# First layer of a four-layer network: transforms beside attention, mixing products beside attention, a late broadcast and weights laid out by the host

## Chip, cores and metric

The kernel runs on one core of one Trainium2 chip. The metric is the device time of one execution in microseconds. The profile shows five engines: PE (TensorE, with its weight loads as PEld), DVE (VectorE), ACT (ScalarE), POOL (GpSimd) and SP (SyncE, which here only issues DMAs). Each engine takes its instructions in the order of its own list; DMAs go through queues that SP, ACT and POOL fill.

## What is computed

The reference is a network of four layers on an input of 4 x 64 images of 128 x 128, each layer a mixing part ("conv") and a second part ("ffn"). The change concerns the mixing part of the first layer, and one constant of the second layer. Cut to what matters:

```python
tokens = x.reshape(B * C, 1, H, W)                # 256 images of 128 x 128
tn = inorm(tokens, n1_g, n1_b)
k, q = fno1(tn, k_spec, k_sw, k_sb, (64, 64)), fno1(tn, q_spec, ...)   # 8 heads, low modes at half size
v = fno1(tn, v_spec, v_sw, v_sb, (128, 128))
attn = softmax(einsum('batm,basm->bats', q, k) / sqrt(m))              # over the 64 images of a batch
out = einsum('bats,basm->batm', attn, v)
a = inorm(fno1(out, p_spec, p_sw, p_sb) + tokens, an_g, an_b)
an = inorm(a, n2_g, n2_b)
h = gelu(inorm(spectral_conv(an, m1_spec)) + conv1x1(an, m1_sw, m1_sb))
h = inorm(spectral_conv(h, m2_spec)) + conv1x1(h, m2_sw, m2_sb)
o = inorm(h, mo_g, mo_b) + a
```

`fno1` is a product of the low Fourier modes with complex weights, plus a pointwise weight; `inorm` normalises an image by its own mean and variance.

## The kernel before

The 256 images are two groups of 128 (two batches each). `l0_conv` (L286) does for each group g first `forward(g)` (L322) and then `attention(g, ...)` (L480), in the order forward(0), attention(0), forward(1), attention(1); the tile scheduler orders the instructions of each engine from this program, and it may start blocks of forward(1) early, where their buffers are free. Then `l0_mixer` (L633) does everything that follows the attention.

`forward(g)` goes over 16 blocks of 8 images. For a block SP loads the images into `xt` (L332, 512 KB); DVE takes their statistics (L179 ff.) and with ACT normalises them into `tt` (L344, L348); POOL's queue writes `tt` to the DRAM tensor `tokens` (L351); PE multiplies each image with the matrix `fx` (L356); ACT copies the low modes to `ylow` (L357) and more modes to `yb` (L358); PE multiplies `yb` with `fg` (L362) and DVE copies the result to `rr` (L366). After the 16 blocks PE makes the low modes in both directions, `c32`, from `ylow` (64 accumulated products), and a Gram matrix from `rr` (32 products, `ghigh`). These two need the whole group.

Once, beside forward(0), small weights of q, k, v and p are loaded on SP's queue, combined by DVE on 8 partitions, written to DRAM (`dq`, `dk`, `dem`) and read back as broadcasts (`wq`, `wk`, later `em`). The constants of the mixer are loaded on SP's queue too, among them four weight tiles `m1_w0` to `m2_w1` (113 x 32): each is set to zero and filled by four DMAs that gather 17 x 32 single elements (L602).

`attention(g)`: 14 DVE products `qt`, `kt` (L491–498); for each of nine heads six transposes on PE, two ACT copies (L509) and three accumulated products (L513), then a DVE operation (L517); softmax (L537–544); sum over heads `ah` (L549); for each of eight value heads one transpose, an ACT copy, six DVE operations (L532–534) and three products (L562); then 16 groups of four transposes of `om` (L579), each copied to `lc` (L581) and written to the DRAM tensor `modes` by POOL's queue; at the end the matrix `mix[g]` (`at2`, L586).

`l0_mixer` works through a list of steps with costs and due times written by hand (class `Plan`), which decides the order on each engine before the kernel is built. `tokens(0)` loads group 0's normalised images from DRAM into `tk0` (4 DMAs of 2 MB), multiplies each of the 128 columns with `mix[0]` (128 products of 128 x 128 x 128 in 32 groups of four, L847) and copies each group of four back into `tk0` (L851, DVE and ACT in turn). `tokens(1)` does the same for group 1 beside the first blocks. Then 16 blocks of 16 images follow: the low modes `lo` are loaded (L870, on SP's queue), inverse transforms (L791, L804) are added (L875), and two spectral convolutions, GELU, normalisations and the residual (`xt`, loaded on SP's queue, L960) make the output `zz`, which POOL's queue writes to `state` (L987).

Ahead of everything else in POOL's order two DMAs on its queue broadcast a constant of 64 KB to 8 MB each in DRAM (`pk`, L3344); the second layer reads `pk`.

Of the kernel before, what the change touches and what calls it, by code (L numbers as in the profile page):

```python
# [22 lines left out]
P = 128  # L23
# [261 lines left out]

def l0_conv(env, x, out, tscr, prm, cst):  # L286

    nc, tc = env.nc, env.tc
    KCH = ((0, 11), (11, 22), (22, 32))
    with ExitStack() as ctx:  # L290
# [11 lines left out]
        def columns(names, n=None):  # L302
            for k in names:
                a = prm[k]
                a = a.rearrange("a b -> (a b)") if len(a.shape) == 2 else a
                sc[k] = cp.tile([P, n or 1], F32, name=k)
                nc.sync.dma_start(sc[k], a.partition_broadcast(P))

        columns(("n1_g", "n1_b"))
        mix = [cp.tile([P, P], F32, name="at2_%d" % g) for g in range(2)]  # L310
        modes = [dram.tile([KR, 64, P], F32, name="modes%d" % g) for g in range(2)]
        with ExitStack() as mctx:
# [8 lines left out]

            def forward(g):  # L322


                i0 = g * P
                NB = 8
                ylow = ap.tile([P, P, 64], F32, name="ylow")
                rr = ap.tile([P, 32, P], F32, name="rr")
                rv = gp.tile([P, P], F32, name="rv")
                for s0 in range(0, P, NB):  # L330
                    xt = bp.tile([P, NB, C], F32, name="xt")
                    nc.sync.dma_start(xt, x[i0 + s0 : i0 + s0 + NB].rearrange("t w c -> w t c"))  # L332
# [18 lines left out]
                    nc.gpsimd.dma_start(tscr[i0 + s0 : i0 + s0 + NB].rearrange("t w c -> w t c"), tt)  # L351
                    yb = bp.tile([P, NB, P], F32, name="yb")
                    for j in range(0, NB, 2):
# [6 lines left out]
                    for k in range(2):  # L360
                        for r in range(2):
# [3 lines left out]
                            )  # L365
                    nc.vector.tensor_copy(rr[:, :, s0 : s0 + NB], p2.rearrange("k t h -> k h t"))  # L366
                alpha = gp.tile([P, P], F32, name="alpha")
                pa = pst.tile([P, P], F32, name="pg")
# [8 lines left out]
                for k0, k1 in KCH:  # L377
                    p3 = psum.tile([P, 11, 34], F32, name="p3", bufs=1)
                    for k in range(k0, k1):
                        nc.tensor.matmul(p3[:, k - k0, :], ylow[:, :, k], fy[:, 0, :], start=True, stop=False)  # L380
                        nc.tensor.matmul(p3[:, k - k0, :], ylow[:, :, 32 + k], fy[:, 1, :], start=False, stop=True)
                    nc.scalar.activation(c32[:, k0:k1, :], p3[:, 0 : k1 - k0, :], AF.Copy, scale=acol)

                nc.vector.tensor_add(c32[:, 0, 0:1], c32[:, 0, 0:1], sc["n1_b"])
# [7 lines left out]
                nc.vector.tensor_scalar(ghigh, ghigh, b64, None, ALU.add)  # L392
                return c32, ghigh, acol

            first = forward(0)


            columns(("p_sb",))
            columns(("q_sw", "k_sw", "v_sw", "p_sw", "q_sb", "k_sb"), 8)
            mask = const(mp, "mask", [P, P])  # L400
# [78 lines left out]

            def attention(g, c32, ghigh, acol):  # L480
                c16 = ap.tile([P, 2, 16, 9], F32, name="c16")
# [8 lines left out]
                for dst, wgt, sb, k in ((qt, wq, "q_sb", 64.0), (kt, wk, "k_sb", 1.0)):  # L490
                    nc.vector.tensor_mul(dst[:, :, 0, :], wgt[:, :, 0, :], cr)  # L491
                    nc.vector.tensor_mul(tmp, wgt[:, :, 1, :], ci)
                    nc.vector.tensor_sub(dst[:, :, 0, :], dst[:, :, 0, :], tmp)
                    nc.vector.tensor_mul(dst[:, :, 1, :], wgt[:, :, 0, :], ci)
                    nc.vector.tensor_mul(tmp, wgt[:, :, 1, :], cr)
                    nc.vector.tensor_add(dst[:, :, 1, :], dst[:, :, 1, :], tmp)
                    d0 = dst[:, 0:8, 0, 0]
                    nc.vector.scalar_tensor_tensor(d0, sc[sb], k, d0, ALU.mult, ALU.add)

                att = ap.tile([P, 8, P], F32, name="att")  # L500
                for h in (8, 0, 1, 2, 3, 4, 5, 6, 7):
                    qk = []
                    for src in (qt, kt):
                        flat = src[:, h].rearrange("p r m -> p (r m)")
                        pt = psum.tile([96, 3, P], F32, name="p1")
                        for j in range(3):
                            nc.tensor.transpose(pt[:, j, :], flat[:, 96 * j : 96 * j + 96], env.ident)
                        t = bp.tile([96, 3, P], F32, name="qkT" + str(len(qk)))
                        nc.scalar.copy(t, pt)  # L509
                        qk.append(t)  # L510
                    psc = psum.tile([P, P], F32, name="p2")
                    for j in range(3):
                        nc.tensor.matmul(psc, qk[0][:, j, :], qk[1][:, j, :], start=(j == 0), stop=(j == 2))  # L513
                    if h == 8:
                        nc.vector.tensor_sub(ghigh, ghigh, psc)
                    else:
                        nc.vector.scalar_tensor_tensor(  # L517
                            att[:, h, :], ghigh, sqsk[:, h : h + 1], psc, ALU.mult, ALU.add
                        )

                fs = []
# [17 lines left out]
                nc.vector.tensor_reduce(mx, att, AX.X, ALU.max)  # L539
                nc.vector.tensor_sub(att, att, mx.unsqueeze(2).to_broadcast([P, 8, P]))  # L540
                nc.scalar.activation(att, att, AF.Exp)
                nc.vector.tensor_reduce(mx, att, AX.X, ALU.add)
                nc.vector.reciprocal(mx, mx)
# [4 lines left out]
                for h in range(1, 8):  # L548
                    nc.vector.scalar_tensor_tensor(ah, att[:, h, :], pv[:, h : h + 1], ah, ALU.mult, ALU.add)  # L549
                rowa = ap.tile([P, 1], F32, name="rowa")  # L550
                nc.vector.tensor_reduce(rowa, ah, AX.X, ALU.add)

                po = [pst.tile([P, 11, 34], F32, name="po%d" % i) for i in range(2)] + [
                    pst.tile([P, 11, 34], F32, name="pg")]
                for h in range(8):
# [5 lines left out]
                    for (k0, k1), o in zip(KCH, po):  # L561
                        nc.tensor.matmul(o[:, 0 : k1 - k0, :], aT, f[:, k0:k1, :], start=(h == 0), stop=(h == 7))  # L562
                om = ap.tile([P, 2, 32, KR], F32, name="om")
                nc.gpsimd.memset(om, 0.0)
# [10 lines left out]
                for r in range(2):  # L575
                    for k0 in range(0, 32, 4):
# [4 lines left out]
                        (nc.scalar.copy if (k0 // 4) % 2 else nc.vector.tensor_copy)(lc, pt)  # L581
                        nc.gpsimd.dma_start(modes[g][:, 32 * r + k0 : 32 * r + k0 + 4, :], lc)

                pt = psum.tile([P, P], F32, name="p1")
                nc.tensor.transpose(pt, ah, env.ident)
                nc.vector.scalar_tensor_tensor(mix[g], pt, acol, env.ident, ALU.mult, ALU.add)  # L586

            attention(0, *first)
            attention(1, *forward(1))


# [4 lines left out]
        for n in ("m1", "m2"):  # L596
            for r in range(2):
                w = cp.tile([KH, 32], F32, name="%s_w%d" % (n, r))
                nc.vector.memset(w, 0.0)
                src = prm[n + "_spec"][0, 0, :, :, r].rearrange("a b -> b a")  # L600
                for q in (0, 32, 64, 96):
                    nc.sync.dma_start(w[q : q + 17, :], src)  # L602

# [25 lines left out]

        l0_mixer(env, x, out, tscr, mix, modes, fx, k, sc)  # L630


def l0_mixer(env, x, out, tscr, mix, modes, fx, k, sc):  # L633

# [7 lines left out]
    with tc.tile_pool(name="l0y", bufs=1) as yp, tc.tile_pool(name="l0m", bufs=DEEP) as sb, tc.tile_pool(name="l0s", bufs=DEEP) as sm, tc.tile_pool(  # L642
# [187 lines left out]
        def tokens(g):  # L830
            tk = yp.tile([P, W, C], F32, name="tk%d" % g)
            plan.block()

            def load(q):
                return lambda: nc.sync.dma_start(
                    tk[:, 32 * q : 32 * q + 32, :], tscr[P * g : P * g + P, 32 * q : 32 * q + 32, :])

            for q in range(4):
                step("sp", 0.1, "", "tk%d" % q, load(q), late=15.0 * (q + 1))

# [19 lines left out]
        def block(g, y, made, s0, par):  # L860
# [10 lines left out]

            step("sp", 0.2, "", "lo", load_modes, new="lo gate", late=4.0)

            def add_low(t0, pb):
# [114 lines left out]

        made = [tokens(0)]  # L990
        for g in range(2):
# [2332 lines left out]
def metaformer(tc, a, out, cst):  # L3324

    with ExitStack() as ctx:
# [14 lines left out]
        f0, f2 = part("L0_ffn_"), part("L2_ffn_")  # L3341
        l0_conv(env, x, state[0], tokens, part("L0_conv_"), cst)
        for g in range(2):
            nc.gpsimd.dma_start(  # L3344
                pk[g][0 : P * W * W, :].rearrange("(t f) o -> t (f o)", t=P), cst["l1c_diag"].partition_broadcast(P)
            )
        rnn_ffn(env, state[0], state[1], f0["W"], f0["VT"], f0["gamma"], f0["beta"])
# [35 lines left out]
```

## Time and profile before

| | |
|---|---|
| median of 3 runs | 12344.46 us (12342.34 to 12349.65) |
| profiled execution: time | 12343.01 us |
| profiled execution: span on the core | 12340.9 us |
| mean granted TensorE clock | 0.786 |
| DVE, ACT, PE, POOL busy over the span | 81%, 61%, 61%, 50% |
| first layer's mixing part | 0 to about 1642 us |
| forward(0): last write to `tokens` issued | 235.86 us |
| attention(1): last DVE operation starts | 603.28 us |
| first low modes added in the mixer (L875) | 722.76 us |
| writes to `state` of the 7th, 8th and 16th block | 1151.00, 1231.08, 1636.59 us |

In a timeline row the columns are the start, the busy time, the engine and line, the operation, the tiles out<-in with their sizes, and in brackets the idle time of the engine before it with what ended it. SPq rows are DMA issues; a merged row of several (x16) spans them all. In a window row the columns are the window and its length, then for each engine the busy time with the number of instructions, the granted TensorE clock (1.00 is full speed), the mean busy share of the DMA engines, and GB/s.

### The profile page before, as it was taken

The numbers are of one execution on the slowest core, as the hardware profiler recorded it, in microseconds if no ns is written. First come the engines' busy times: TensorE is split into PE (matmuls) and PEld (weight loads), VectorE is DVE, ScalarE is ACT, GpSimd is POOL, SyncE is SP. The second block draws the span as 40 slices with busy tenths as digits, with TensorE's granted clock in tenths as the row PEclk, the third lists the DMA queues.
The fourth block names the chain that finished last, engine by engine and source line by source line (L and its number), as shares of the span: only waits on it lengthen the run. The fifth ranks groups of instructions, "written<-read, shape, count | busy, mean of one in ns | idle before, by whom it ended". The sixth has DMA issues, their size and how long they took to land. (4 is left out here: it accounts for less than half of the span.)

```text
span 12340.9 us, 115256 instructions
## 1 busy us (share of the span) xinstructions
PE 7507.1 (61%) x34606; PEld 4559.4 (37%) x34606; DVE 10011.8 (81%) x16345; ACT 7567.9 (61%) x10926; POOL 6178.9 (50%) x5275
## 2 busy tenths in 40 slices
PE   4677778100000000008899799999999999998765
PEld 3465555100000000007788444444444444445443
DVE  4546645899999999997778599999999999997354
ACT  2245553588886777732233477787787877876342
POOL 0100013799991000002222499998998999995222
PEclk7787789655555555559999899999999999999877
DMA  4221125311111111111111133333333333333434
GB/s 138 90 62 41 42 95 168 90 57 58 57 59 53 56 56 53 52 40 44 37 42 37 67 137 140 140 137 139 138 144 136 140 139 138 136 139 118 180 121 153
DMA packets 640569, 1193.52 MB, mean 97 GB/s; under 512 B 224772, under 2 KB 442166, under 8 KB 560566
## 3 DMA queue, kind: packets, MB, share of 16 engines
q1 hardware_dynamic: 598454, 1043.00, 25.3%
q0 software_dynamic: 34656, 140.92, 3.5%
q8 instruction: 279, 4.57, 0.2%
q14 instruction: 364, 2.98, 0.1%
q10 hardware_dynamic: 6816, 2.05, 0.1%
HBM read 950.84 MB, written 251.71 MB: 97 GB/s over the span
## 5 line engine op out<-in xcount | busy, mean ns | idle before, releaser
L2655 POOL TENSOR_TENSOR gs<-hist,cc 128x512 f32<-128x512 f32 x2048 | 2572.2, 1264 | 379.6 <-DVE hist L2650 218.5
L2650 DVE TENSOR_TENSOR_SCAN hist<-da,state,bs 128x512 f32<-128x512 f32 x1984 | 2519.4, 1270 | 0.0
L2664 PE MATMUL py<-gs,ident 128*128 128x512 f32 x4096 | 2242.2, 630 | 6.0 <-DVE y L2540 6.0
L1589 PE MATMUL pt<-ident,both 128*128 128x128 f32 x6 | 2.7, 447 | 3257.3 <-DMA pk<-spare 3185.6
L2621 ACT ACTIVATE da<-dt,am 128x512 f32<-128x512 f32 x2048 | 1419.2, 717 | 320.6 <-DVE hist L2650 316.8
L2642 DVE TENSOR_TENSOR bs<-dx,bs 128x512 f32<-128x512 f32 x2048 | 1389.3, 678 | 185.4 <-PE bs L2628 140.6
L1465 POOL TENSOR_TENSOR diff<-key 128x2048 f32<-128x2048 f32 (+11 forms) x364 | 1384.2, 3856 | 86.4 <-DVE key L1470 75.0
L1589 PEld LDWEIGHTS pt<-ident,both 128*128 128x128 f32 x6 | 1.1, 182 | 3258.8 <-issue 3258.8
L2664 PEld LDWEIGHTS py<-gs,ident 128*128 128x128 f32 x4096 | 739.1, 197 | 901.4 <-issue 428.8
L1849 POOL IOTA places<- 128x128 int32 x1 | 0.2, 239 | 1812.1 <-SPq L1789 1812.1
L2628 PE MATMUL bs<-bt,pick 96*128 96x512 bf16 x2048 | 806.6, 394 | 139.3 <-DVE hist L2650 136.5
L1487 ACT COPY keep<-rank 128x1536 int16<-128x1536 int16 (+11 forms) x364 | 613.4, 1688 | 436.7 <-DVE rank L1489 387.8
L1463 ACT COPY low<-key 128x2048 f32<-128x2048 f32 (+11 forms) x364 | 627.7, 1725 | 284.2 <-DVE key L1470 275.4
L1488 DVE COPY_PREDICATED rank<-back,rank 128x1536 int16<-128x1536 uint8 (+11 forms) x364 | 781.2, 2146 | 16.8 <-ACT keep L1487 16.8
L1489 DVE COPY_PREDICATED rank<-back,keep 128x1536 int16<-128x1536 uint8 (+11 forms) x364 | 777.7, 2136 | 12.5
L1470 DVE TENSOR_TENSOR key<-low,key 128x2048 f32<-128x2048 f32 (+11 forms) x364 | 744.3, 2045 | 12.4
L1469 DVE TENSOR_TENSOR key<-low,key 128x2048 f32<-128x2048 f32 (+11 forms) x364 | 748.8, 2057 | 6.8 <-DMA key<-dist 6.1
L1466 ACT ACTIVATE turned<-diff 128x2048 int8<-128x2048 f32 (+11 forms) x364 | 600.6, 1699 | 36.2 <-DMA key<-dist 28.0
L1478 ACT ACTIVATE back<-turned 128x3072 uint8<-128x3072 int8 (+12 forms) x182 | 582.6, 3201 | 0.0
L2121 PE MATMUL pe<-ew,xg 128*128 128x128 f32 x4096 | 534.4, 284 | 1.5 <-DVE xg L2103 1.5
L987 POOL DMA_DIRECT2D state<-zz x16 | 18.5, 1156 | 1015.2 <-DVE zz L977 593.1
L2121 PEld LDWEIGHTS pe<-ew,xg 128*128 128x128 f32 x4096 | 484.6, 194 | 33.8 <-DVE xg L2103 2.3
(812 smaller groups left out, 18815.2 us busy)
## 6 DMA issues: line engine op xcount, KB each, us to landing
cc<-cd SPq DMA_DIRECT2D x512, 1024.0 KB
xt<-state SPq DMA_DIRECT2D x64, 1024.0 KB
xo<-state SPq DMA_DIRECT2D x128, 256.0 KB
state<-xo POOLq DMA_DIRECT2D x128, 256.0 KB, 2.9
xl<-in_L_ffn_weight SPq DMA_DIRECT2D x32, 1024.0 KB
xt<-in_x SPq DMA_DIRECT2D x32, 512.0 KB
tokens<-tt POOLq DMA_DIRECT2D x32, 512.0 KB, 5.0
tk<-tokens SPq DMA_DIRECT2D x8, 2048.0 KB
```

The lines of the kernel that those rows point to most:

```text
L1465: nc.gpsimd.tensor_sub(d, lo[part], hi[part])
L1469: nc.vector.tensor_tensor(lo[part], c, hi[part], ALU.min)
L1470: nc.vector.tensor_tensor(hi[part], c, hi[part], ALU.max)
L1488: nc.vector.copy_predicated(l, t, h)
L1489: nc.vector.copy_predicated(h, t, kv)
L2121: T.matmul(w["pe"][:, j, :], w["xg"][:, q, j, :], ew[:, q, :], start=False, stop=(q == E - 1))
L2621: nc.scalar.activation(da, x_["dt%d" % b], AF.Exp, scale=am[:, s : s + 1])
L2628: nc.tensor.matmul(bs, pick[:, s, :], x_["bt%d" % b], start=True, stop=True)
L2642: nc.vector.tensor_mul(db, x_["dx%d" % b], db)
L2650: nc.vector.tensor_tensor_scan(h, live.pop(("da", t)), live.pop(("db", t)), 0.0 if first else state[b][:, s : s + 1], ALU.mult, ALU.add,)
L2655: nc.gpsimd.tensor_tensor(gs, h, live.pop(("cc", t)), ALU.mult)
L2664: nc.tensor.matmul(x_["py%d" % b], env.ident, live.pop(("gs", t)), start=(s == 0), stop=(s == S - 1))
```

## The change

1. `forward` and `attention` become generators that yield after each piece. `beside(a, b, late)` draws from both in turn: attention(0) beside forward(1), and attention(1) beside the mixing products of group 0 (`mixing()`), the latter after the first 0.3 of the steps.
2. A tile `tk0` of 64 KB per partition is kept from the start to the end. During the two forwards it holds `ylow`, `rr` and both buffers of `xt` and `yb`; after forward(1) group 0's tokens are loaded into it. The matrix `mix[g]` is made ahead of the value heads.
3. `tokens(1)` is planned behind the loads of `lo` of the first block.
4. The two broadcasts to `pk` become a step of the mixer on POOL (`aside`), in the plan behind the load of `lo` of the second block of group 1.
5. The host lays out the weights of the two spectral convolutions (`m1_specL`, `m2_specL`), so that each tile is one contiguous load without a preceding zero fill.
6. The loads of `columns` (19 small broadcasts) are issued by ACT in place of SP, and those of the attention stand ahead of forward(0).

```diff
-                nc.sync.dma_start(sc[k], a.partition_broadcast(P))
-        columns(("n1_g", "n1_b"))
+                nc.scalar.dma_start(sc[k], a.partition_broadcast(P))
+        columns(("n1_g", "n1_b", "p_sb"))
+        columns(("q_sw", "k_sw", "v_sw", "p_sw", "q_sb", "k_sb"), 8)
         mix = [cp.tile([P, P], F32, name="at2_%d" % g) for g in range(2)]
+        tk0 = cp.tile([P, W, C], F32, name="tk0")
+        flat = tk0.rearrange("p w c -> p (w c)")
+        ylow = flat[:, 0 : 64 * P].rearrange("p (t k) -> p t k", k=64)
+        rr = flat[:, 64 * P : 96 * P].rearrange("p (h t) -> p h t", t=P)
+        turned = flat[:, 96 * P :].rearrange("p (i s t c) -> i s p t c", i=2, s=2, t=8)
...
-            def forward(g):
+            def forward(g, made):
...
-                    xt = bp.tile([P, NB, C], F32, name="xt")
+                    xt, yb = turned[s0 // NB % 2]
...
                     nc.vector.tensor_copy(rr[:, :, s0 : s0 + NB], p2.rearrange("k t h -> k h t"))
+                    yield
...
+            def beside(a, b, late=0.0):
+                a, b = iter(a), iter(b)
+                for i in range(STEPS):
+                    next(a, None)
+                    for _ in range(int(max(i + 1 - late * STEPS, 0) * 32 / (STEPS - late * STEPS))
+                                   - int(max(i - late * STEPS, 0) * 32 / (STEPS - late * STEPS))):
+                        next(b, None)
+                for rest in (a, b):
+                    for _ in rest:
+                        pass
+
+            def mixing():
+                for c0 in range(0, C, 4):
+                    pm = psum.tile([P, 4, P], F32, name="p1")
+                    for j in range(4):
+                        nc.tensor.matmul(pm[:, j, :], tk0[:, :, c0 + j], mix[0], start=True, stop=True)
+                    eng = nc.scalar.copy if (c0 // 4) % 2 else nc.vector.tensor_copy
+                    eng(tk0[:, :, c0 : c0 + 4].rearrange("w t c -> w c t"), pm)
+                    yield
+
+            STEPS = 48
+            first, second = [], []
+            for _ in forward(0, first):
+                pass
...
-            attention(0, *first)
-            attention(1, *forward(1))
+            beside(attention(0, first), forward(1, second))
+            for q in range(0, W, 32):
+                nc.sync.dma_start(tk0[:, q : q + 32, :], tscr[0:P, q : q + 32, :])
+            beside(attention(1, second), mixing(), 0.3)
...
                 w = cp.tile([KH, 32], F32, name="%s_w%d" % (n, r))
-                nc.vector.memset(w, 0.0)
-                src = prm[n + "_spec"][0, 0, :, :, r].rearrange("a b -> b a")
-                for q in (0, 32, 64, 96):
-                    nc.sync.dma_start(w[q : q + 17, :], src)
+                nc.sync.dma_start(w, prm[n + "_specL"][r])
...
-            plan.block()
+            plan.block("lo")
...
-                step("sp", 0.1, "", "tk%d" % q, load(q), late=15.0 * (q + 1))
+                step("sp", 0.1, "lo", "tk%d" % q, load(q), late=15.0 * (q + 1))
...
             step("sp", 0.2, "", "lo", load_modes, new="lo gate", late=4.0)
+            if g == 1 and s0 == NB:
+                step("pool", 2.0, "lo", "", aside)
...
-        made = [tokens(0)]
+        made = [(y0, {})]
...
-        l0_conv(env, x, state[0], tokens, part("L0_conv_"), cst)
-        for g in range(2):
-            nc.gpsimd.dma_start(
-                pk[g][0 : P * W * W, :].rearrange("(t f) o -> t (f o)", t=P), cst["l1c_diag"].partition_broadcast(P)
-            )
+        def diagonals():
+            for g in range(2):
+                nc.gpsimd.dma_start(
+                    pk[g][0 : P * W * W, :].rearrange("(t f) o -> t (f o)", t=P), cst["l1c_diag"].partition_broadcast(P)
+                )
+        l0_conv(env, x, state[0], tokens, part("L0_conv_"), cst, diagonals)
```

More of the change, by code (lines that the diff above doesn't have):

```diff
@@ L283, in symmetrize, with l0_conv @@
     return s
-def l0_conv(env, x, out, tscr, prm, cst):
+def l0_conv(env, x, out, tscr, prm, cst, aside):
     nc, tc = env.nc, env.tc
@@ L320, in l0_conv @@
             fg = const(mp, "fg", [P, 2, 64])
-            def forward(g):
+            def forward(g, made):
                 i0 = g * P
                 NB = 8
-                ylow = ap.tile([P, P, 64], F32, name="ylow")
-                rr = ap.tile([P, 32, P], F32, name="rr")
                 rv = gp.tile([P, P], F32, name="rv")
                 for s0 in range(0, P, NB):
-                    xt = bp.tile([P, NB, C], F32, name="xt")
+                    xt, yb = turned[s0 // NB % 2]
                     nc.sync.dma_start(xt, x[i0 + s0 : i0 + s0 + NB].rearrange("t w c -> w t c"))
@@ L351, in forward @@
                     nc.gpsimd.dma_start(tscr[i0 + s0 : i0 + s0 + NB].rearrange("t w c -> w t c"), tt)
-                    yb = bp.tile([P, NB, P], F32, name="yb")
                     for j in range(0, NB, 2):
@@ L392, in forward @@
                 nc.vector.tensor_scalar(ghigh, ghigh, b64, None, ALU.add)
[L393 to L399, printed above, removed]
+                made.extend((c32, ghigh, acol))
+            def beside(a, b, late=0.0):
[15 more added lines that the diff above has]
+                    eng(tk0[:, :, c0 : c0 + 4].rearrange("w t c -> w c t"), pm)
+                    yield
+            STEPS = 48
+            first, second = [], []
+            for _ in forward(0, first):
+                pass
             mask = const(mp, "mask", [P, P])
@@ L478, in l0_conv, with attention @@
             wq, wk = wqk
-            def attention(g, c32, ghigh, acol):
+            def attention(g, made):
+                c32, ghigh, acol = made
                 c16 = ap.tile([P, 2, 16, 9], F32, name="c16")
@@ L491, in attention @@
                     nc.vector.tensor_mul(dst[:, :, 0, :], wgt[:, :, 0, :], cr)
+                    yield
                     nc.vector.tensor_mul(tmp, wgt[:, :, 1, :], ci)
                     nc.vector.tensor_sub(dst[:, :, 0, :], dst[:, :, 0, :], tmp)
+                    yield
                     nc.vector.tensor_mul(dst[:, :, 1, :], wgt[:, :, 0, :], ci)
                     nc.vector.tensor_mul(tmp, wgt[:, :, 1, :], cr)
+                    yield
                     nc.vector.tensor_add(dst[:, :, 1, :], dst[:, :, 1, :], tmp)
@@ L498, in attention @@
                     nc.vector.scalar_tensor_tensor(d0, sc[sb], k, d0, ALU.mult, ALU.add)
+                    yield
                 att = ap.tile([P, 8, P], F32, name="att")
@@ L519, in attention @@
                         )
+                    yield
                 fs = []
@@ L540, in attention @@
                 nc.vector.tensor_sub(att, att, mx.unsqueeze(2).to_broadcast([P, 8, P]))
+                yield
                 nc.scalar.activation(att, att, AF.Exp)
+                yield
                 nc.vector.tensor_reduce(mx, att, AX.X, ALU.add)
@@ L549, in attention @@
                     nc.vector.scalar_tensor_tensor(ah, att[:, h, :], pv[:, h : h + 1], ah, ALU.mult, ALU.add)
+                    if h % 4 == 3:
+                        yield
                 rowa = ap.tile([P, 1], F32, name="rowa")
                 nc.vector.tensor_reduce(rowa, ah, AX.X, ALU.add)
+                pt = psum.tile([P, P], F32, name="p1")
+                nc.tensor.transpose(pt, ah, env.ident)
+                nc.vector.scalar_tensor_tensor(mix[g], pt, acol, env.ident, ALU.mult, ALU.add)
                 po = [pst.tile([P, 11, 34], F32, name="po%d" % i) for i in range(2)] + [
@@ L562, in attention @@
                         nc.tensor.matmul(o[:, 0 : k1 - k0, :], aT, f[:, k0:k1, :], start=(h == 0), stop=(h == 7))
+                    yield
                 om = ap.tile([P, 2, 32, KR], F32, name="om")
@@ L582, in attention @@
                         nc.gpsimd.dma_start(modes[g][:, 32 * r + k0 : 32 * r + k0 + 4, :], lc)
-                pt = psum.tile([P, P], F32, name="p1")
-                nc.tensor.transpose(pt, ah, env.ident)
-                nc.vector.scalar_tensor_tensor(mix[g], pt, acol, env.ident, ALU.mult, ALU.add)
-            attention(0, *first)
-            attention(1, *forward(1))
+                        if k0 % 8:
+                            yield
+            beside(attention(0, first), forward(1, second))
+            for q in range(0, W, 32):
+                nc.sync.dma_start(tk0[:, q : q + 32, :], tscr[0:P, q : q + 32, :])
+            beside(attention(1, second), mixing(), 0.3)
         columns(("an_g", "an_b", "n2_g", "n2_b", "mo_g", "mo_b", "m1_sw", "m1_sb", "m2_sw", "m2_sb"))
@@ L628, in l0_conv, with l0_mixer @@
         nc.vector.tensor_add(k["c0"], sc["an_b"], sc["mo_b"])
-        l0_mixer(env, x, out, tscr, mix, modes, fx, k, sc)
-def l0_mixer(env, x, out, tscr, mix, modes, fx, k, sc):
+        l0_mixer(env, x, out, tscr, mix, modes, fx, k, sc, tk0, aside)
+def l0_mixer(env, x, out, tscr, mix, modes, fx, k, sc, y0, aside):
     nc, tc = env.nc, env.tc
@@ L3372 @@
         laid[name + "T" * t] = np.ascontiguousarray(np.asarray(v).T if t else v)
+        if name in ("L0_conv_m1_spec", "L0_conv_m2_spec"):
+            m = np.zeros((2, KH, 32), np.float32)
+            for q in (0, 32, 64, 96):
+                m[:, q : q + 17] = np.asarray(v)[0, 0].transpose(2, 1, 0)
+            laid[name + "L"] = m
+            del laid[name]
     arrays, aps = {}, {}
```

## The prediction, made before the changed kernel was run

> **What bounds the kernel now.** I read the 40 slices of the page first: the first layer's mixing part is the first five slices (0–1642 us), and the change touches nothing behind it, so only these slices count. There DVE is busy 4 to 6 tenths; nothing is saturated, so waits set the time. I then cut the stretch into windows of 25 us and read, in each empty window, the timeline of the engine that stands still.
>
> ```profile
> core 0: us, PE busy (x) PEld busy (x) DVE busy (x) ACT busy (x) POOL busy (x), PEclk, DMA share, GB/s
> 125.00:150.00 25.00, 0.00 (x0) 0.00 (x0) 3.22 (x31) 0.00 (x0) 0.00 (x0) 0.50 0.09 1
> 200.00:225.00 25.00, 16.83 (x96) 12.09 (x96) 20.53 (x115) 14.75 (x48) 3.54 (x4) 1.00 0.55 179
> 325.00:350.00 25.00, 16.75 (x43) 8.99 (x43) 22.46 (x34) 1.51 (x6) 0.00 (x0) 0.85 0.33 113
> 475.00:500.00 25.00, 25.00 (x117) 25.00 (x117) 0.83 (x6) 1.70 (x3) 0.00 (x0) 0.50 0.00 1
> 600.00:625.00 25.00, 1.96 (x8) 1.20 (x6) 1.03 (x2) 0.58 (x1) 1.84 (x4) 0.50 0.79 319
> ```
>
> The first row is a window in which no engine works; the second is the forward transform running freely; the third is attention's value heads (DVE bound, PE 2/3); in the fourth PE alone works (the c32 and gram products); in the fifth only the DMAs do. The timelines say why:
>
> ```profile
> 3.88 0.73 POOL L3344 DMA_DIRECT2D pk<-in_l1c_diag  x1
> 36.42 0.17 DVE L403 TENSOR_TENSOR sqsk<-q_sw,k_sw 128x8 f32<-128x8 f32 x1 [25.02 <-DMA k_sw<-in_L_conv_k_sw]
> 43.93 0.56 POOL L3344 DMA_DIRECT2D pk<-in_l1c_diag  x1
> 104.23 56.01 SPq L602 DMA_DIRECT2D m_w<-in_L_conv_m_spec  x16
> 166.99 0.89 POOL L351 DMA_DIRECT2D tokens<-tt  x1 [73.10 <-DVE tt L348]
> 235.86 0.89 POOL L351 DMA_DIRECT2D tokens<-tt  x1 [6.53 <-ACT yb L358]
> 667.42 1.02 DVE L851 COPY tk<-p 128x512 f32<-128x512 f32 x1 [63.79 <-PE p L847]
> 665.20 61.75 PE L847 MATMUL p<-at,tk 128*128 128x128 f32 x280
> ```
>
> The 4 KB of k_sw, issued at 5.83, are awaited until 36.42, while pk (8 MB, "35.5" us to land) is under way. The 16 gathers occupy SP's queue for 56 us, and the x load stands behind them. So group 0's last tokens go out at 235.86. At 603.6 attention ends; DVE then idles 63.79 us while 16 MB of tokens land and the first products run.
>
> **Part by part.** *Start.* Freely running, forward puts out a block every 6.2 us (token writes from 383.65 to 457.62, 12 intervals), of which DVE is busy 5.0 us (20.53 of 25). With pk and the gathers gone from here, and the m_spec weights one contiguous load each (four issues of about 0.43 us, as the other constants), the last of 16 blocks comes at: first write about 19 us (x landed and DVE began at 7.66; statistics, root and normalising until about 12; a few us for ACT, which now issues 16 small loads first, 16 × 0.43 = 7 us, in place of SP), plus 15 × 6.2 = 93, plus the weight set-up, whose DVE work is about 21 us, partly in the slack of 1.2 us per block: 14. Sum 126. **Gain 236 − 126 = 110** (95 with the set-up's DMA round trips exposed, 120 with it hidden). The column loads on ACT's queue cost nothing beyond the 7 us: they hide in the first x load.
>
> *c32(0)+gram(0)*: 237–278, 41 us, not touched. Two blocks of forward(1) already run there.
>
> *Stage 2*, from 271 (DVE's first qt) to 507 (end of c32(1)+gram(1)) = 236 us: attention(0) 105, 14 blocks 90, c32(1) 41. The change interleaves the first two. DVE's work adds: 14 × 5.0 = 70 plus attention's 71 (the windows from 275 to 375). PE's new order starts c32(1) between value heads 3 and 4, so four heads (4 × 6 × 0.72 = 17) and the closing copies (7) fall beside c32(1): 117 remain on the path. At the share that DVE reaches where it has work, 22.46/25 = 0.90, that is 130 us. c32(1) gets company on a PE that was full: 41 + value heads 12 (16.75 of 25 us for 6.3 heads) + six pairs of om transposes at 1.95 = 65. Sum 195: **gain 41** (65 if that PE work finds holes; 15 if the order stalls, DVE at 0.75).
>
> A rule on this row: TensorE's granted clock is 0.50 in the fourth window with PE 25 of 25 us busy, and I price c32(1) at that row. The Trainium skill ("TensorE: Matmul & The Clock Gate", Part 1) says the clock is halved only after idle windows and full after about 3.4 us of sustained work; by it the 41 us would be about 21 and the sum 20 us lower. The row contradicts it.
>
> *Stage 3*, from 499.6 (first qt of attention(1)) to the first add_low at 722.8 = 223 us: attention 104, loads 61.6, products 57. Now group 0's 8 MB load (half of what took 59 us, so about 27–30) lies beside the om tail, qt/kt (27 us) and heads (21). A group of four products takes 1.76 us of PE (2 groups per 3.51), and of the 32 groups 2 stand among the heads, 4 in the softmax, 7 among the value heads, 8 among the om pairs, 11 after the end. Softmax 11, value heads 36 (before 32), om 8 pairs × 4 us (3.24 now, of which PE is idle 1.29 and gets 1.76 more; DVE's wait of 2.55 per pair for modes<-lc covers the 1.02 us copies), 11 × 1.76 = 19: 27 + 21 + 11 + 36 + 32 + 19 = 146. Against it: the lo loads and the first inverse after the pools are freed, 6 (before they hid in the load); group 1's products, later in the mixer, 5; three more for copies behind DVE's waits. **Gain 77 − 14 = 63** (35 if products run at half clock, 0.88 us each as they do beside a clock of 0.50; 80).
>
> *pk in the mixer.* POOL issues both after the 7th block's output and before the 8th. The DMA issues (median to landing), POOL's timeline and a window in the gap:
>
> ```profile
> pk<-in_l1c_diag POOLq DMA_DIRECT2D x2, 35.5
> ```
>
> ```profile
> 1151.00 1.16 POOL L987 DMA_DIRECT2D state<-zz  x1 [28.64 <-DVE ka L889]
> 1231.08 1.15 POOL L987 DMA_DIRECT2D state<-zz  x1 [78.91 <-DVE zz L977]
> ```
>
> ```profile
> 1186.00:1201.00 15.00, 10.57 (x54) 5.92 (x51) 5.45 (x19) 11.12 (x24) 0.00 (x0) 0.61 0.00 0
> ```
>
> Blocks come in pairs, 29 and 77 us apart; in the long gap the DMA share is 0.04 to 0.00 from 1156 to 1216. Two transfers of 31–35.5 us last 62–71 us, to about 1223. In it falls one x load (issued about 1220, needed at 1224.5): late by up to 9. POOL does nothing else in that stretch; its next write comes at 1231. I take 4 us; ends 0 and 71 (all of it exposed). For 71 speaks k_sw's row: its 4 KB came only when pk had landed.
>
> A rule on that row: the Trainium skill ("DMA: Bandwidth & Descriptors", Queues, rings and completion order) has each DMA engine take turns between queues packet by packet. In the first 60 us pk's queue moved 13.57 MB in 495 packets (27 KB each), SP's 2.45 MB in 6212 (394 B each); by the rule, loads of such small packets starve beside pk, and the sum would hold all of the overlap with the mixer's loads, at most the 71.
>
> Sum: 110 + 41 + 63 − 4 = **210 us**. The profiled execution is 12343.0 (span 12340.9, 2.1 around it), so 12133; the median of the runs is 1.5 above it: 12134.5.
>
> **Rivals.** *A: the interleaving brings nothing.* DVE and PE take their work in order, and the p1 buffers (two) are now shared by heads, blocks and products; each chain may wait for the other's. Stage 2 stays 236 (gain 0); stage 3 is 104 + 32 × 1.76 = 160 plus 14: gain 49. Sum 110 + 0 + 49 − 4 = 155: 12189.5. For it: heads now run as chains PE–ACT–PE of 1.88 us with DVE waiting. Against: DVE has 5.0 us of independent work per block to put into these waits. *B: pk starves the mixer.* If x, lo and the output write stand still for the whole 71 us: 12134.5 + 67 = 12201.5. For it: k_sw's row; against: the empty stretch above. *C: one tile, coarse waits.* xt, yb, ylow and rr now share the tile tk0. Were each x load held until the last reader of the block before (in place of the buffer two before), a block would be a chain: load 4.6 us (issued 3.08, first statistics 7.66) + statistics to rr copy 10.1 (406.41 to 416.49) = 14.7 in place of 6.2. Group 0 then costs 16 × 8.5 = 136 more; in stage 2 attention's pieces stand in the chain too: 16 × 14.7 + 71 + 41 = 347 instead of 195, 152 more. Net −210 + 288 = 78 slower: 12422. It decides from 210/32 = 6.6 us per block on. For it: the order does not tell which event a wait names. Against: the writes of ylow carry no wait for another engine, and an x load waits for DVE and ACT, as in the kernel before.
>
> **How the numbers follow.** Forecast 0.65, A 0.16, B 0.11, C 0.08. What can be told from no change is 0.2%, 25 us. Forecast, A and B are all faster by over 100; C reaches from a little faster to 100 slower. Faster 0.90, same 0.03, slower 0.07. The range takes the upper gains 120 + 65 + 80 − 0 = 265 (12079.5) and reaches past B's 12201.5 to 95 + 15 + 35 − 12 = 133 (12211.5).
>
> **What would show it.** Right: token writes every 6 us from about 19 us, the 16th near 126, no gap of 56 us on SP; between the end of gram(0) and that of gram(1) 190 us with DVE near 0.9; first add_low near 722 − 215 = 507; seven outputs 210 us earlier and the 8th 75–85 us after the 7th. Wrong: block intervals of 12 us or more (C); DVE at 0.6 beside attention(0) (A); an 8th output 130 us or more after the 7th (B).

## The result, and the profile after

The changed kernel takes 12121.97 us (median of 4 runs, 12118.02 to 12133.7) against 12347.06 us (4 runs): a ratio of 0.9819 with a 95% interval of 0.9802 to 0.9836. The forecast was 12134.5. The profiled execution has a span of 12123.1 us, 217.8 less than before; its landmarks, in us:

| | before | after | earlier by | forecast |
|---|---|---|---|---|
| 16th write to `tokens` | 235.9 | 127.4 | 108.5 | 110 |
| gram(1) read by DVE (`ghigh`) | 506.9 | 355.1 | 151.8 | 151 |
| first added low modes | 722.8 | 509.6 | 213.2 | 214 |
| first output | 834.0 | 617.8 | 216.2 | |
| 7th output | 1151.0 | 949.1 | 201.9 | |
| 8th output | 1231.1 | 1017.3 | 213.8 | |
| 16th output | 1636.6 | 1414.6 | 222.0 | 210 |

These are DMA issues on POOL and instructions on DVE; from one kernel to another with the same start the 16th write lies between 124.1 and 127.4, so differences under some 3 us are not read.

The windows of the changed kernel that answer to those shown before (a free forward block, forward beside attention(0), c32(1) in company, the products behind attention(1)):

```profile
core 0: us, PE busy (x) PEld busy (x) DVE busy (x) ACT busy (x) POOL busy (x), PEclk, DMA share, GB/s
100.00:125.00 25.00, 18.21 (x96) 13.76 (x96) 19.97 (x113) 14.67 (x49) 3.54 (x4) 0.93 0.52 169
225.00:250.00 25.00, 23.48 (x152) 18.15 (x150) 21.47 (x110) 17.33 (x55) 3.54 (x4) 1.00 0.53 169
325.00:350.00 25.00, 24.63 (x119) 24.14 (x120) 3.67 (x13) 2.82 (x5) 2.06 (x4) 0.61 0.10 29
475.00:500.00 25.00, 23.66 (x116) 23.03 (x116) 7.33 (x8) 6.80 (x8) 3.11 (x6) 1.00 0.48 119
```

The empty windows are gone: at 125–150 us, where PE stood still before, group 0's c32 runs. Beside attention(0) DVE is busy 0.84 to 0.91 of the time (windows from 175 to 275 us), PE up to 0.94. POOL's and DVE's timelines:

```profile
127.37 0.90 POOL L357 DMA_DIRECT2D tokens<-tt  x1 [5.51 <-ACT tk L362]
355.05 0.35 DVE L396 SCALAR_TENSOR_TENSOR ghigh<-pg,acol,alpha 128x128 f32<-128x128 f32 x1 [1.24 <-PE pg L394]
509.62 1.29 DVE L919 TENSOR_TENSOR tk<-tk,pb 128x512 f32<-128x512 f32 x2 [6.59 <-PE pb L846]
949.06 1.16 POOL L1031 DMA_DIRECT2D state<-zz  x1 [53.21 <-DVE zz L1021]
950.21 1.09 POOL L3389 DMA_DIRECT2D pk<-in_l1c_diag  x2
1013.78 1.14 DVE L1008 SCALAR_TENSOR_TENSOR xt<-tk,ka,xt 128x128 f32<-128x128 f32 x4 [18.15 <-DMA xt<-in_x]
1017.29 1.18 POOL L1031 DMA_DIRECT2D state<-zz  x1 [65.98 <-DVE zz L1021]
```

From the 4th to the 12th the outputs now follow one another evenly, about 54 us apart, where they came in pairs 29 to 31 and 77 to 82 us apart. Among these only the 8th is late: the residual waits 18.15 us for its x load.

### The profile page after: what moved, and what is told of

It is laid out like the page before. It is cut to its first block, busy times and chain, and to the rows that moved or that the text cites. A ratio compares the mean times of both kernels' runs of the same rounds, so it can differ in the third digit from the quotient of the medians.

```text
span 12123.1 us, 115274 instructions
## 1 busy us (share of the span) xinstructions
PE 7529.4 (62%) x34606; PEld 4567.5 (38%) x34606; DVE 10007.7 (83%) x16341; ACT 7550.9 (62%) x10927; POOL 6180.6 (51%) x5275
## 3 DMA queue, kind: packets, MB, share of 16 engines
q1 hardware_dynamic: 587454, 1042.99, 25.7%
## 5 line engine op out<-in xcount | busy, mean ns | idle before, releaser
L1533 DVE COPY_PREDICATED rank<-back,keep 128x1536 int16<-128x1536 uint8 (+11 forms) x364 | 777.9, 2137 | 12.5
L2147 POOL TENSOR_TENSOR xg<-xT,gr 128x512 f32<-128x512 f32 x192 | 245.3, 1278 | 473.1 <-ACT gr L2143 472.9
```

The source lines that it names most:

```text
L1533: nc.vector.copy_predicated(h, t, kv)
```

## The experiments

The first four take back one part of the change each.

**pk at the start again.**

```diff
-            if g == 1 and s0 == NB:
-                step("pool", 2.0, "lo", "", aside)
...
+        diagonals()          # behind l0_conv, as before; it comes first in POOL's order
```

> The changed kernel with the two broadcasts to pk back at the start, at the head of POOL's queue; nothing else differs. Theory: at the start they starve the small loads (k_sw waited 25 us for them in the kernel before), in the mixer they cost about the 14 us by which the 8th output follows later than the usual 54 us. So the 16th write to tokens comes 45 to 65 us later than 127.4, the gap between the 7th and 8th output shrinks from 68 to 54 us, and the time rises by 30 to 50 us. Rival B (pk costs in the mixer what it costs at the start): the time stays within 10 us.

12176.94 us (ratio to before 0.9863, 0.9846 to 0.9879): 55 us longer than the change, a little more than the 30 to 50 expected. The 16th write comes at 189.5, 62 us later; the 7th and 8th output are 54.3 us apart; the 16th output comes 45.8 us later. DVE's timeline of this run:

```profile
37.26 0.17 DVE L434 TENSOR_TENSOR pv<-p_sw,v_sw 128x8 f32<-128x8 f32 x1 [27.22 <-DMA p_sw<-in_L_conv_p_sw]
82.56 1.64 DVE L179 BATCH_NORM_STATS2 ln_st<-tk 128x6 f32<-128x128 f32 x8 [28.76 <-DMA tk<-in_x]
1059.17 1.14 DVE L1006 SCALAR_TENSOR_TENSOR xt<-tk,ka,xt 128x128 f32<-128x128 f32 x4 [4.63 <-DMA xt<-in_x]
```

Each of the two broadcasts costs one wait of 27 to 29 us at the start (POOL issues the second only at 49.22 us, behind two writes to `tokens`), and without them the residual waits 4.63 us instead of 18.15. The same transfers cost 62 us at the start and 14 in the mixer: rival B falls.

**Stage 2 in turn.**

```diff
-            beside(attention(0, first), forward(1, second))
+            for _ in attention(0, first): pass
+            for _ in forward(1, second): pass
```

> The changed kernel with attention(0) and forward(1) one after the other; the rest as changed. Theory: the interleaving brought 41 to 44 us, so gram(1) ends 41 to 55 us later than 354.7 (up to two blocks that ran beside c32(0) may add 12), and the time rises by the same. Rival A (interleaving brings nothing, the gain of the stage came from the faster start): within 10 us.

12154.3 us, 32 longer. `ghigh` of group 1 is made at 396.7, 41.6 us later; the 16th output 35.7 later. From the `--source` view of this line (duration of its two instructions in ns, then their starts in us):

```profile
L396 DVE SCALAR_TENSOR_TENSOR ghigh<-pg,acol,alpha x2: 349/350/351, 168.1 to 396.7; 128x128 f32<-128x128 f32 x2
```

At gram(1) the interleaving is worth what the forecast said, and rival A falls for this stage. Not all of it reaches the end: the time was expected to rise by 41 to 55 us, and at the first added low modes (542.9) the run is 33 us behind. In the change some copies to `lc` of attention(0) still run among the first products of attention(1), and from `ghigh` to the next use of it (L550) 25.7 us pass, against 16.3 here.

**Products behind attention(1).**

```diff
-            beside(attention(1, second), mixing(), 0.3)
+            for _ in attention(1, second): pass
+            for _ in mixing(): pass
```

> The changed kernel with the mixing products of group 0 all behind attention(1), the load of their tokens still beside it. Theory: of the 63 us of the third stage about 60 come from the hidden load, only about 14 from the products: the first added low modes come 8 to 20 us later than 509.6, the time rises as much. Rival: the products are the gain (57 us of them stood alone before): 35 us or more.

12145.01 us, 23 longer; first added low modes at 522.8 (13.2 later), 16th output 13.5 later. Of the 61 us of the third stage 48 remain without the interleaving. They are put down to the tokens' loads (group 0's 8 MB beside attention, group 1's behind the first `lo`), which before held DVE for 63.79 us; no run takes these loads back alone, or tells the two apart.

**Gathered weights.**

```diff
-                nc.sync.dma_start(w, prm[n + "_specL"][r])
+                nc.vector.memset(w, 0.0)
+                src = prm[n + "_spec"][0, 0, :, :, r].rearrange("a b -> b a")
+                for q in (0, 32, 64, 96):
+                    nc.sync.dma_start(w[q : q + 17, :], src)
```

> The changed kernel with the weights m1 and m2 gathered again by 16 element-wise loads on SP's queue. Theory: SP is held 56 us, x loads stand behind, the 16th write to tokens comes 40 to 55 us later than 127.4, and the time rises by 40 to 55 us. Rival (the gathers fall into the waits of the weight set-up and only pk was costly): under 15 us.

12170.19 us; 16th write at 169.0 (41.6 later), 16th output 44.3 later. SP's queue in this run:

```profile
58.57 23.47 SPq L647 DMA_DIRECT2D m_w<-in_L_conv_m_spec  x6
82.15 3.28 SPq L338 DMA_DIRECT2D tk<-in_x  x1
85.47 5.43 SPq L647 DMA_DIRECT2D m_w<-in_L_conv_m_spec  x2
```

SP spends 2.5 us on a gather (median of the 16, from 0.25 to 7.9; 40 us in all, 56 in the kernel before), and x loads come between them, at 82 and 100 us for instance. So of the 108.5 us of the start, 62 fall to pk and 42 to the gathers, each measured by taking it back alone.

**Columns on SP's queue** (`nc.sync` for `nc.scalar` in `columns`).

> The changed kernel with the small column loads on SP's queue again. Theory: nine of them, 0.45 us each, now stand ahead of the first x load on SP, so the first write to tokens comes 3 to 8 us later than 18.9 and everything behind keeps that; nothing else moves. Rival (the columns on ACT's queue hold up the first normalisation as much as they would the x load): the first write comes within 2 us of 18.9.

One run: first write at 21.0 (2.2 later), 16th at 131.8 (4.5 later), 16th output 8.2 later. Between the two expectations at the first write; a few us in all.

**One buffer for xt and yb** (`turned[0]` for `turned[s0 // NB % 2]`).

> The changed kernel with one buffer for xt and yb in place of two, which puts a price on rival C. By C's working a block is then a chain of 14.7 us in place of 6.2: the 16th write to tokens near 240 to 265 in place of 127, the time about 200 to 300 us longer. If the chain is shorter than worked out (the load waits only for xt's readers, which end well ahead of the block's last step): blocks of 9 to 11 us, 60 to 130 us longer.

12254.13 us (ratio 0.9927, 0.9910 to 0.9943): 132 us longer than the changed kernel, but still faster than before. POOL's timeline:

```profile
141.14 0.89 POOL L357 DMA_DIRECT2D tokens<-tt  x1 [11.03 <-DVE tt L354]
150.61 0.89 POOL L357 DMA_DIRECT2D tokens<-tt  x1 [8.58 <-ACT tk L362]
160.16 0.89 POOL L357 DMA_DIRECT2D tokens<-tt  x1 [8.66 <-DVE tt L354]
170.14 0.89 POOL L357 DMA_DIRECT2D tokens<-tt  x1 [9.10 <-DVE tt L354]
```

SP's waits between 60 and 180 us (us in total, times, longest) name what holds the loads:

```profile
SPq L338 <- DVE tt L354: 99.2, 12, 11.5
```

A block takes 10, not 14.7 us: the load waits for the normalisation that reads xt, not for the block's last step.

**pk one block apart** (step at `s0 in (NB, 2 * NB)`, one broadcast each).

> The changed kernel with the two broadcasts to pk issued one block apart (after the 7th and after the 8th output) in place of both after the 7th. Theory: one broadcast lasts 33 us and fits the quiet 44 us between the loads of two blocks; the 18.15 us wait of DVE for xt shrinks to the 4.6 us it is without pk, the 7th, 8th and 9th output are 54 to 56 us apart (68.2 and 53.6 now), and the 16th output comes 10 to 14 us earlier than 1414.6. Rival (the cost is one of contention, whenever pk moves): both gaps grow by about 7 us and the sum stays.

12115.97 us (ratio 0.9816, 0.9799 to 0.9832). The times can't tell this from the change; the timeline can:

```profile
946.96 1.16 POOL L1031 DMA_DIRECT2D state<-zz  x1 [52.86 <-DVE zz L1021]
948.11 0.56 POOL L3388 DMA_DIRECT2D pk<-in_l1c_diag  x1
999.98 1.18 POOL L1031 DMA_DIRECT2D state<-zz  x1 [51.30 <-DVE zz L1021]
1001.15 0.56 POOL L3388 DMA_DIRECT2D pk<-in_l1c_diag  x1
1054.04 1.17 POOL L1031 DMA_DIRECT2D state<-zz  x1 [52.33 <-DVE zz L1021]
```

Gaps of 53 and 54 us, waits for xt of 4.6 and 4.4 us, first to 16th output 784.1 us (796.8 in the change). A broadcast that fits the quiet stretch costs nothing that shows here, and the rival (both gaps 7 us longer) falls.

**Products of group 0 as steps of the plan** (`made = [tokens(0)]` again, working on the kept `tk0`, without its loads).

> The changed kernel with the products of group 0 as steps at the head of the mixer's plan again (their tokens loaded early as in the change), which is to show where the 20 us come from by which the mixer, from its first to its 16th output and without pk, is shorter than before (783 against 803 us). Theory: the even spacing of the blocks (54 us, before pairs of 29 and 77 us) comes from the plan no longer beginning with these products; then here the pairs return and the stretch from first to 16th output is 795 to 820 us with pk, and the first added low modes come 10 to 25 us later than 509.6. Rival (the spacing comes from the late load of group 1's tokens): even spacing, 797 us.

One run, 12154.23 us: the first low modes come at 518.4 (8.8 later, where 10 to 25 were expected), the 16th output 23.2 later, first to 16th output take 811.8 us, and the pairs are back:

```profile
948.98 1.16 POOL L1032 DMA_DIRECT2D state<-zz  x1 [28.11 <-DVE ka L934]
950.13 1.09 POOL L3390 DMA_DIRECT2D pk<-in_l1c_diag  x2
1028.75 1.19 POOL L1032 DMA_DIRECT2D state<-zz  x1 [77.53 <-DVE zz L1022]
1057.54 1.17 POOL L1032 DMA_DIRECT2D state<-zz  x1 [27.60 <-DVE ka L934]
```

In the long gap of 80 us both broadcasts find room, and the 8th output is not late (80.1 us before, without pk). The products alone, behind attention(1) but outside the plan, don't bring the pairs back: in the run "Products behind attention(1)" the outputs stay about 54 us apart.

**Wide c32**: 102 streamed columns, in eight parts.

```diff
+            for i in range(3): nc.vector.tensor_copy(fyw[:, :, i, :], fy)
-                for k0, k1 in KCH:
+                for k0, k1 in [(i, i + 4) for i in range(0, 32, 4)]:
...                 # fyw (128 x 102) in place of fy (128 x 34)
```

> The changed kernel in which the c32 products stream 102 columns (the 34 of fy three times side by side) in place of 34, in eight parts in place of three; one of the three equal copies is kept, so the values are the same. It asks why the granted clock is 0.50 in this stage although PE is busy throughout. If the clock follows how much the array streams and not whether instructions are under way, it rises well above 0.50 in the stage, each product falls from 0.41 to about 0.28 us, and c32(0)+gram(0) falls from 41 us to 30 to 36 (with eight waits for ACT). If the clock is held down for another reason, it stays at 0.50 and the stage takes 45 us or more.

**The same eight parts with 34 columns.**

> The changed kernel with the c32 products in eight parts, but 34 columns as in the change: which of the two made the last output 18 us earlier when 102 columns were streamed? If it was the clock (1.00 in place of 0.50), the clock is 0.50 here and gram(1) ends at 353 to 357, the 16th output within 5 us of 1414.6. If it was the finer parts (blocks of forward(1) and the attention find more places between them), the second write of group 1 comes near 143 in place of 174 and most of the 18 us are here too.

One run each: 12121.87 and 12115.44 us, too near to the change to be told apart by time. At the 16th output the wide version is 17.9 us earlier than the change, the eight parts alone 9.9 later; their `ghigh`(1) comes at 370.0, 15 later, which neither expectation had. Windows of the wide version, then of the change, then of the eight parts with 34 columns:

```profile
145.00:152.00 7.00, 7.00 (x40) 7.00 (x39) 1.82 (x13) 0.94 (x3) 0.00 (x0) 1.00 0.31 112
152.00:159.00 7.00, 7.00 (x39) 7.00 (x39) 2.60 (x18) 0.94 (x3) 0.00 (x0) 1.00 0.00 1
```

```profile
145.00:152.00 7.00, 7.00 (x34) 7.00 (x34) 0.66 (x7) 0.00 (x0) 0.89 (x1) 0.50 0.46 150
152.00:159.00 7.00, 7.00 (x34) 7.00 (x33) 1.65 (x9) 0.76 (x2) 0.00 (x0) 0.50 0.00 0
```

```profile
145.00:152.00 7.00, 7.00 (x35) 7.00 (x34) 4.59 (x26) 1.70 (x5) 0.00 (x0) 0.50 0.14 51
152.00:159.00 7.00, 7.00 (x34) 7.00 (x33) 0.00 (x0) 0.75 (x2) 0.89 (x1) 0.50 0.33 99
```

And PE's timeline of the wide version, then of the change (a product shows as two records, so a row of x2 is one product; `pg` rows are Gram products):

```profile
332.77 0.60 PE L391 MATMUL p<-fyw,tk 128*128 128x102 f32 x2
333.20 0.60 PE L390 MATMUL p<-fyw,tk 128*128 128x102 f32 x2
342.23 4.41 PE L398 MATMUL pg<-tk 128*128 128x128 f32 x38
```

```profile
335.26 0.62 PE L386 MATMUL p<-fy,tk 128*128 128x34 f32 x2
335.69 0.62 PE L387 MATMUL p<-fy,tk 128*128 128x34 f32 x2
336.99 2.48 PE L394 MATMUL pg<-tk 128*128 128x128 f32 x10
```

The granted clock doubles, and the eight parts alone leave it at 0.50; but a c32 product starts every 0.43 us in both, where 0.28 was expected. The kernel before shows the same with 34 columns at both clocks: its c32(1) begins at a clock of 1.00, which holds until 472 us, and is at 0.50 from 473 on:

```profile
470.99 0.60 PE L380 MATMUL p<-fy,ylow 128*128 128x34 f32 x2
471.43 0.60 PE L381 MATMUL p<-fy,ylow 128*128 128x34 f32 x2
474.48 0.62 PE L380 MATMUL p<-fy,ylow 128*128 128x34 f32 x2
474.91 0.63 PE L381 MATMUL p<-fy,ylow 128*128 128x34 f32 x2
```

What got faster are the neighbours, the Gram products among them (0.12 us a record against 0.25 in the rows above): from the first c32 product to `ghigh`(0) 36.7 us in place of 40.3, `ghigh`(1) 7.7 us earlier, the first low modes 16.2.

**All together, first without the wide c32** (`mixing()` without the 0.3, pk apart), **then with it.**

> The version with pk one block apart, and the mixing products beside all of attention(1) in place of from 0.3 of its steps on. Theory: fewer groups of products are left behind attention(1) (7 or 8 in place of 11), so the first added low modes come 0 to 8 us earlier than 507.8 and the rest as in the version with pk apart. Rival (the early products delay the heads as much as they shorten the end): within 2 us, or later.

One run, 12111.17 us: first low modes at 504.4 (3.4 earlier than with pk apart), 16th output at 1389.9, 10.8 us earlier than with pk apart; where the other 7 us come from stays open.

> All that the runs pointed to: the changed kernel with pk one block apart, the products beside all of attention(1), and the c32 products streaming 102 columns in eight parts. If the gains at the last output add up (14 from pk, 11 from the earlier products, 18 from the wide c32), the 16th output comes near 1372 in place of 1414.6, and the time near 12080, a ratio of 0.978 to 0.980 to the kernel before.

12094.21 us (5 runs, 12076.91 to 12116.08), ratio to before 0.9794 (0.9781 to 0.9807). The 16th output comes at 1395.1, 19.5 earlier than in the change, not the 42 of the sum (the profile is that of the longest of the five, 12116.08 us). The median is 28 us below the change's, but the two intervals overlap (to 0.9807, from 0.9802). The gain that does not add is that of the wide c32: without it the 16th output came at 1389.9. With it the first low modes are 6 us earlier (498.2), and the stretch from there to the 16th output 11 us longer (896.9 against 885.5); why stays open.

## Why the prediction was right

*The start* (110, measured 108.5): both mechanisms hold, and taken back alone they cost 62 and 42 us. The trace of before could only give their sum.

*Stage 2* (41, measured 43.3 between the landmarks, 41.6 when taken back). The pieces are right too: DVE is busy 0.88 of the 130 us from 162 to 292, where 0.90 and 130 us were put, and c32(1) with its company on PE, priced at the row of before, took 63 us for 65. Of this gain 33 us are left at the first low modes.

*Stage 3* (63, measured 61.4): 13 from the interleaved products and, by what is left, 48 from the loads. Its lower bound (35) had no ground: products at a clock of 0.50 don't take 0.88 us each. In the kernel before the copies of the first groups of four, at 0.50, start 1.6 to 1.7 us apart (667.42, 669.12 and 670.76), no further than at 1.00 (1.76).

*pk* (4, measured 14) is the mis-sized term. The mechanism is the one described, the x load issued late in the gap, but the gap was taken from a row of before (77 us), and the changed plan has none: 44 us lie between two rounds of loads, and the two transfers, which keep the DMA engines busy until about 1007, 57 us, do not fit. The 8th output was to come 75 to 85 us after the 7th and comes 68 after it. With the pairs back the two broadcasts cost nothing visible; 4 us had been put.

*The mixer's rhythm* is the term that was missing. From the first low modes to the 16th output the kernel before takes 913.8 us, the changed kernel with pk at the start 892.0: 22 us that the sum did not have. Putting group 0's products back into the plan brings pairs and 919.4 us. So the plan's order, not the load of group 1's tokens, makes the spacing. The spacing is not the whole gain, though: of the 19.5 us by which the stretch from first to 16th output is shorter than before (783.1 with pk at the start, for 802.6), 12 lie behind the 12th output (181.3 for 193.6) and 7 between the 2nd and the 12th; why stays open. These 22 us and pk's 10 too many partly offset each other, which is luck: the gain came out 12 us larger than forecast at the 16th output (222 for 210), and the median 12.5 us below the forecast.

*Rivals.* A and B fall with the runs above. C did not happen: from the 11th on blocks are 5.7 to 7.1 us apart, 6.2 on average. Its price was too high as well: with one buffer a block costs 10 us, and the kernel stays 90 us faster than before; the chain was worked out to the block's last step, where the load waits only for the normalisation that reads xt. A wait for the whole tile itself was not tried.

*The rules.* The Trainium skill's clock rule ("TensorE: Matmul & The Clock Gate", Part 1) would have made the c32 stage 20 us shorter; in the change the rows of c32(0) stay at 0.50 with PE busy throughout. That full clock would bring those 20 us is wrong too: at 1.00 the products keep their pace. The skill's rule of turns by packet ("DMA: Bandwidth & Descriptors", Queues, rings and completion order) agrees with both places: loads of small packets beside a broadcast wait 18 to 29 us, in the mixer as at the start, and the cost was the larger where more of them fell beside it (62 and 14 us).

## What to carry to other kernels

A large transfer without urgency costs what it overlaps: look for the stretch without loads, and measure that stretch in the order of the changed kernel, since a plan that starts differently may space its blocks differently. Loads of single elements hold the queue that issues them, and everything behind it, however few bytes they move (16 of them 40 to 56 us here). Where two stages have complementary engines, a sum of the bound engine's work at the share it reaches elsewhere (here 0.90) gave the gain of the stage within 3 us.

## What was not expected of the hardware

In these runs the granted TensorE clock goes with how much is streamed, not with whether PE is busy: 0.50 with 34 columns per product and 1.00 with 102, in eight parts both times, with PE busy 7.00 of 7.00 us in both. And the clock did not set the pace of these products: 0.43 us each at 0.50 and at 1.00, with a weight load of 310 and 312 ns (median) for `ylow`, whose columns lie 64 elements apart. The Gram products, whose weights from `rr` are contiguous, do follow the clock: weight loads of 333 ns at 0.50 and 192 ns at 1.00. That the spacing of the weights is the cause was not tried.
